# Cross-attention and quantised feed-forward: the order of two score products within a step

## The chip, the cores and the metric

The kernel runs on one core of a Trainium2 chip. The metric is the device time of one execution in microseconds (us); "before" is the median of three runs. PE is TensorE, DVE is VectorE, ACT is ScalarE, POOL is GpSimd, and SP is the queue that issues most transfers.

## The reference

The inputs are `x` and a context `ctx`, both 4 x 1024 x 512 in float32. What is computed, cut to what matters:

```
# per batch, N = 1024 tokens (768 image, then 256 text), 16 heads of 32
q = layernorm(x) @ Wq + bq;  k = ctx @ Wk + bk;  v = ctx @ Wv + bv
scores = q k^T / sqrt(32)
# mask: an image token sees its own third of the image (256 tokens);
#       a text token sees all the image and, causally, the text
attn = softmax(scores);  x = x + (attn @ v) @ Wo + bo
# feed-forward with fake quantisation to 8 bits of activations (one scale for
# the whole tensor) and of weights (one scale for each row), inner width 1408
x = x + down( quant( silu(gate(quant(layernorm(x)))) * up(...) ) )
```

## The kernel before

The program has three stages. Attention with its projections is the first, up to about 870 us of the span; the gate and up products of the feed-forward, up to about 1032 us, are the second; the down products are the third. The change lies in the first stage alone.

**Units and steps.** Queries are worked on in blocks of 256 tokens, and heads in four groups `g` of four. A `Unit` is one block of queries against one block of 256 keys, for one group of heads. An image block has one unit for each group; a text block has four (its `part` 0 to 3), since it looks at all four key blocks. There are 112 units. The main loop (lines 821 to 908) runs over steps `n`, and each step works on three units in a software pipeline:

- `maxima(units[n])` (lines 426 to 449) makes scores `s` with the queries on the partitions: eight products into four PSUM banks, one for each head of the group. DVE then takes the row maxima of each bank (L445 for image blocks, L449 for text blocks, after adding a mask at L448 where the block is causal). They become the shifts of the softmax: POOL rounds them to pairs of bf16 (`minus_maxima`, L465 and L466), and a transposing transfer lays them along the free axis (`shifts`, L473, tile `nmT`).
- `weights(units[n - T_LAG], ...)` (lines 476 to 516), five units behind, makes the scores once more with the keys on the partitions. Four small bf16 products (L488) put minus the maxima into four banks `t`, and eight products (L492) add the scores. ACT takes the exponentials (L494) into `pT`. The function that it returns, `sums`, adds them up on POOL (L514).
- `values(units[n - V_LAG])` (lines 518 to 572), six units behind, multiplies `pT` of the step before with the values (L532, bank `av`), and at the last part with a block of ones for the sums (L555).
- `large(n)` then does one larger piece: half of a projection of a coming block (tiles `pp_q`, `pp_kv`, `pv`) or of an output projection (`po`), all at L225. Its bank is called the large bank below. From step `LATE` on the pieces are half as large.

After these come, on DVE, whatever the step has of background work: the reciprocal of the sums (L567), a sum of terms for text blocks (L569 and L545), taking an output projection (L588) and its statistics (L595 to L598), the statistics of a new query block (L359, L360), scales of the weights of the feed-forward (L636 to L638), and the transposition of a new block of inputs (L260).

**What sets the order.** For PE, DVE, ACT and POOL the order is the program's own: `tc.manual_schedule` (line 777) takes the instructions of each engine as they are written. The transfers of SP are placed by the scheduler. So the order in which PE meets the products of one step is the order of the calls in the loop: `weights`, `maxima`, `values`, `large`.

**Banks.** All PSUM of the stage is one pool of eight banks with one tag:

```python
        def bank(name):
            return ps_b.tile([P, 512], F32, tag="b", name=name)
```

A step takes ten banks: four for `s`, four for `t`, one for `av`, one for the large piece. A product that takes a bank has to wait until its last reader, from the tile that held the bank before, is done. In the built program the bank numbers go round: almost always a tile takes the bank that was taken eight tiles earlier.

Of the kernel before, what the change touches and what calls it, by code (L numbers as in the profile page):

```python
# [42 lines left out]
def kernel(ctx: ExitStack, tc: tile.TileContext, x, kv, Wq, bq, Wk, bk, Wv, bv, Wo, bo, clip_x, clip_down, w_gate, w_up, w_down, out):  # L43
# [78 lines left out]
    with ExitStack() as actx:  # L122
# [9 lines left out]
        def bank(name):  # L132
            return ps_b.tile([P, 512], F32, tag="b", name=name)
# [267 lines left out]
        def rows_of(j):  # L401
            return slice(j * D, (j + 1) * D)
# [23 lines left out]
        def maxima(u):  # L426

            k, g = u.k, u.g
            q = Q[k.c]
            if u.part == 0:  # L430
                state[k.n, g] = small.tile([P, 4, 2, 2], F32, tag="nmh", name=f"nmh_{u.n}", bufs=4)
            nmh = state[k.n, g]
            s = [bank(f"s_{u.n}_{j}") for j in range(4)]
            i, half = u.part // 2, u.part % 2
            n = 2 * QB - (P if k.text and half and i == 0 else 0)
            for m in range(2):
                if k.text:
                    key, rows, w = K[k.keys[2 * half + m]], slice(i * P, (i + 1) * P), min(QB, n - m * QB)
                else:
                    key, rows, w = K[k.c], slice(m * P, (m + 1) * P), QB  # L440
                for j in range(4):
                    nc.tensor.matmul(s[j][:, m * QB : m * QB + w], q[rows_of(j), g, rows], key[rows_of(j), g, :w], start=True, stop=True)  # L442
            for j in range(4):
                if not k.text:
                    nc.vector.tensor_reduce(nmh[:, j, :, 0], s[j].rearrange("p (i q) -> p i q", i=2), AX.X, ALU.max, negate=True)  # L445
                    continue
                if half:
                    nc.vector.tensor_tensor(s[j][:, n - P : n], s[j][:, n - P : n], mask, ALU.add)  # L448
                nc.vector.tensor_reduce(nmh[:, j, i, half : half + 1], s[j][:, :n], AX.X, ALU.max, negate=True)  # L449
# [3 lines left out]
        def minus_maxima(u):  # L453

            k, g = u.k, u.g
            nmh = state.pop((k.n, g))
            if k.text:
                nm = small.tile([P, 4, 2], F32, tag="nm", name=f"nm_{u.n}")
                nc.vector.tensor_reduce(nm, nmh, AX.X, ALU.min)
            else:  # L460
                nm = nmh[:, :, :, 0]
            nm = nm.rearrange("p j i -> p i j")
            nm2 = nm2s[turn[0] % NMB]
            turn[0] += 1
            nc.gpsimd.tensor_copy(nm2[:, :, :, 0], nm)  # L465
            nc.gpsimd.tensor_tensor(nm2[:, :, :, 1], nm, nm2[:, :, :, 0], ALU.subtract)  # L466
            u.nm2 = nm2

        def shifts(u):

            k, g, nm2 = u.k, u.g, u.nm2
            nmT = nmp.tile([P, QB], BF16, tag="nmT", name=f"nmT_{u.n}")
            nc.sync.dma_start_transpose(nmT.rearrange("p (i q) -> p i q", i=2), nm2.rearrange("p i j d -> p (i j d)"))  # L473
            state["T", k.n, g] = nmT
# [176 lines left out]
        units = []  # L651
# [33 lines left out]
        def can_small(n):  # L685
            return at_small < len(jobs) and at_small <= at_big + 1 and prepared.get(at_small, n) < n
# [36 lines left out]
        def need_rows(kind, c, g, n):  # L723

            while rows_done.get((kind, c), 0) <= g:
                advance(n)

        def need_values(c, n):
            while ("v", c) not in done:
                advance(n)  # L730
# [9 lines left out]
        def step_output(half=False):  # L740
            outputs[0].step(half)
            if outputs[0].i == 2:
                outputs.pop(0)
                for o in outputs[:2]:
                    o.load()

        def finished(k):
            outputs.append(Output(k))
            for o in outputs[:2]:
                o.load()  # L750
# [70 lines left out]
        for n in range(len(units) + V_LAG):  # L821
            previous = units[n - 1] if 0 < n <= len(units) else None
            if n < len(units):
                u = units[n]
                half = u.part % 2
                for c in u.k.keys[2 * half : 2 * half + 2] if u.k.text else u.k.keys:
                    need_rows("k", c, u.g, n)
                need_rows("q", u.k.c, u.g, n)

            def shifts_of_previous():  # L830
                if previous is not None and previous.part == previous.parts - 1:
                    shifts(previous)

            if T_LAG <= n < len(units) + T_LAG:
                sums = weights(units[n - T_LAG], shifts_of_previous)
            else:
                shifts_of_previous()
                sums = None
            if n < len(units):
                maxima(u)  # L840
            if sums is not None:
                sums()
            if n < len(units) and u.part == u.parts - 1:
                minus_maxima(u)
            if n in (2, 3, 4, 5):
                (spread, sigmoids, product, total)[n - 2]()

            for first, c in ((True, (n - 5) // 3), (False, (n - 7) // 3)):
                rows = slice(c * QB, (c + 1) * QB)
                if not 0 <= c < B * NQB or (n - (5 if first else 7)) % 3:  # L850
                    continue
                if first:
                    nc.sync.dma_start(x1_d[rows, :].rearrange("(t p) c -> p t c", p=P), bo_b.unsqueeze(1).to_broadcast([P, QB // P, C]))
                else:
                    nc.gpsimd.dma_start(x1_d[rows, :], x_tok[rows, :], accum_op=ALU.add, max_dma_last_dim=C)
            t = units[n - T_LAG] if T_LAG <= n < LATE else None
            crowded = t is not None and t.k.text and t.part > 1
            while sum(b.__name__ == "moments" for b in background) > 1:
                background.popleft()()
            f = background.popleft() if background and n > 0 and not (crowded and background[0].__name__ == "deviation") else None  # L860
            if f is not None and f.__name__ in ("deviation", "apply", "quantise"):
                f()
                f = background.popleft() if background and f.__name__ == "quantise" else None
            fs = list(later)
            later.clear()
            for g in fs:
                g()
            ends = None
            if n >= V_LAG:
                v = units[n - V_LAG]  # L870
                need_values(v.k.keys[v.part], n)
                if v.part == 0 and v.g == 0:
                    while len(outputs) + len(whole) >= OUTS:
                        step_output()
                if v is units[-5]:
                    tail.load()
                ends = values(v)
            if ends is not None:
                avs, av, quotient = ends
                if n < len(units) + V_LAG - 1:  # L880
                    nc.scalar.copy(avs, av)
            large(n)
            while whole:
                finished(whole.pop(0))
            if f is not None:
                f()
            if ends is not None and n < len(units) + V_LAG - 1:
                later.append(quotient)
            if n == len(units) + V_LAG - 2:
                assert not outputs  # L890
                tail_products(0, (0, 1))

            if weight_stages and quantised[0]:
                weight_stages.popleft()()
            if can_small(n):
                small_step()
            prepare_next(n)
            if n > n_img and n_weights < 2 * NIC and not weight_stages and len(background) < 2:
                stages = weight_unit(n_weights)
                background.extend(stages[:2])  # L900
                weight_stages.append(stages[2])
                n_weights += 1
            if n < LATE and spent + BIG < target(n) and can_big(n + 1):
                big_step()
            if n >= V_LAG:
                u = units[n - V_LAG]
                if u.part == u.parts - 1 and u.g == NCC - 1 and u is not units[-1]:
                    whole.append(u.k)
# [306 lines left out]
```

## Time and profile before

| what | value |
|---|---|
| median of three runs | 1118.52 us (1116.16 to 1120.01) |
| the profiled execution's own time | 1117.18 us |
| its span, first to last instruction | 1115.3 us |
| mean granted TensorE clock | 0.987 |
| PE busy | 1087.0 us, 97% of the span |
| DVE busy | 846.9 us, 76% |
| ACT busy | 522.1 us, 47% |
| POOL busy | 531.0 us, 48% |

The profile has a page of busy times, groups of instructions by source line, and a chain of work that ended last; the trace behind it can be asked for the instructions of an engine in order of time. A row of the timeline gives the start in us, the time taken, the engine, the line, the operation, what it writes and reads, and the number of instructions merged into the row. In brackets stands idle time of the engine before it, with what ended it. A product in float32 is recorded as two matmuls, so the eight products of `s` appear as sixteen. The table by windows gives for each stretch of time the busy time of each engine and, after the engines, the granted clock of PE as a share of full speed.

### The profile page before, as it was taken

The numbers are of one execution on the slowest core, as the hardware profiler recorded it, in microseconds if no ns is written. First come the engines' busy times: TensorE is split into PE (matmuls) and PEld (weight loads), VectorE is DVE, ScalarE is ACT, GpSimd is POOL, SyncE is SP. The second block draws the span as 40 slices with busy tenths as digits, with TensorE's granted clock in tenths as the row PEclk, the third lists the DMA queues.
The fourth block names the chain that finished last, engine by engine and source line by source line (L and its number), as shares of the span: only waits on it lengthen the run. The fifth ranks groups of instructions, "written<-read, shape, count | busy, mean of one in ns | idle before, by whom it ended". The sixth has DMA issues, their size and how long they took to land.

```text
span 1115.3 us, 32159 instructions
## 1 busy us (share of the span) xinstructions
PE 1087.0 (97%) x13851; PEld 585.9 (53%) x13851; DVE 846.9 (76%) x1316; ACT 522.1 (47%) x941; POOL 531.0 (48%) x615
## 2 busy tenths in 40 slices
PE   9998999999999999999999999989999899998998
PEld 5555555465655555565545556655554344443444
DVE  2555678797688959778786887987777788877887
ACT  3344444354445435454533455554443565553653
POOL 1224447678764567775446666765642221110110
PEclk9998999999999999999999999998999899999999
DMA  7369636355645454332222122212211698311895
GB/s 236 93 202 284 144 80 133 72 117 102 121 63 115 94 117 85 108 82 65 92 73 67 42 77 61 60 53 80 72 66 58 203 287 247 75 34 39 300 382 193
DMA packets 138262, 135.91 MB, mean 122 GB/s; under 512 B 56060, under 2 KB 103432, under 8 KB 136712
## 3 DMA queue, kind: packets, MB, share of 16 engines
q1 hardware_dynamic: 115600, 91.91, 29.6%
q0 software_dynamic: 22208, 41.42, 14.1%
q8 instruction: 108, 1.77, 0.7%
q10 hardware_dynamic: 312, 0.53, 0.2%
q14 instruction: 34, 0.28, 0.1%
HBM read 79.96 MB, written 50.07 MB: 117 GB/s over the span
## 4 chain that ended last, share of the span: by engine, by line
PE 81%; DMA 6%; DVE 5%; POOL 3%; issue 2%; ACT 2%; SPq 1%; DVEq 0%; POOLq 0%; ACTq 0%
PE po L225 9%; PE av L532 8%; PE pv L225 8%; PE pp_q L225 8%; PE pp_kv L225 8%; PE s L442 8%; PE t L492 7%; PE pg L1055 7%; PE pu L1055 7%; PE t L488 3%; PE av L555 3%; PE pd L1158 2%; POOL sp L514 2%; DMA xt<-x_d 2%; ACT pT L494 1%
## 5 line engine op out<-in xcount | busy, mean ns | idle before, releaser
L494 ACT ACTIVATE pT<-t 128x512 f32<-128x512 f32 x448 | 231.3, 603 | 135.7 <-PE t L492 135.5
L514 POOL TENSOR_TENSOR sp<-pT 128x1024 f32<-128x1024 f32 x59 | 140.8, 2386 | 173.8 <-ACT pT L494 173.7
L514 POOL TENSOR_TENSOR sp<-sp,pT 128x1024 f32<-128x1024 f32 x84 | 188.8, 2248 | 46.8 <-ACT pT L494 43.5
L449 DVE TENSOR_REDUCE nmh<-s 128x1 f32<-128x512 f32 (+1 forms) x256 | 159.2, 655 | 46.7 <-PE s L442 42.3
L445 DVE TENSOR_REDUCE nmh<-s 128x2 f32<-128x512 f32 x192 | 119.0, 683 | 58.9 <-PE s L442 58.9
L442 PE MATMUL s<-kT,qT 32*128 32x256 f32 (+1 forms) x1792 | 128.5, 376 | 3.1 <-DVE xr L588 2.5
L532 PE MATMUL av<-pT,va 128*32 128x256 f32 (+1 forms) x1792 | 118.9, 383 | 1.7 <-ACT pT L494 1.4
L225 PE MATMUL pp_q<-qT,Wq_sb 128*32 128x256 f32 x2048 | 117.4, 379 | 0.0
L225 PE MATMUL pv<-Wv_sb,kvT 128*32 128x512 f32 (+1 forms) x1088 | 116.3, 567 | 0.0
L492 PE MATMUL t<-qT,kT 32*128 32x256 f32 (+1 forms) x1792 | 115.1, 371 | 0.0
L225 PE MATMUL po<-Wo_sb,oT 128*32 128x512 f32 (+1 forms) x1120 | 110.9, 536 | 0.0
L567 DVE RECIPROCAL avs<-avs 128x256 f32<-128x256 f32 x63 | 109.9, 1744 | 0.0
L225 PE MATMUL pp_kv<-kvT,Wk_sb 128*32 128x256 f32 x1920 | 109.0, 379 | 0.0
L442 PEld LDWEIGHTS s<-kT,qT 32*128 32x128 f32 x1792 | 99.0, 187 | 16.1 <-DVE xr L588 3.4
L492 PEld LDWEIGHTS t<-qT,kT 32*128 32x128 f32 x1792 | 89.6, 186 | 7.2 <-issue 0.7
L1055 PE MATMUL pg<-xqT,wgT 128*128 128x512 bf16 x352 | 91.0, 382 | 0.5 <-DVE xqT L1016 0.5
L225 PEld LDWEIGHTS pp_q<-qT,Wq_sb 128*32 128x32 f32 x2048 | 67.7, 110 | 44.9 <-issue 3.6
L1055 PE MATMUL pu<-xqT,wuT 128*128 128x512 bf16 x352 | 90.6, 381 | 0.0
L1061 ACT ACTIVATE silu<-pg,sg 128x512 f32<-128x512 f32 x88 | 60.0, 686 | 64.9 <-PE pg L1055 64.9
L1082 DVE SCALAR_TENSOR_TENSOR h<-pu,su,silu 128x512 f32<-128x512 f32 x88 | 65.4, 747 | 30.2 <-PE pu L1055 29.2
L225 PEld LDWEIGHTS pp_kv<-kvT,Wk_sb 128*32 128x32 f32 x1920 | 63.8, 110 | 42.7 <-issue 4.5
L532 PEld LDWEIGHTS av<-pT,va 128*32 128x32 f32 x1792 | 48.6, 110 | 56.7 <-ACT pT L494 27.2
(190 smaller groups left out, 1340.5 us busy)
## 6 DMA issues: line engine op xcount, KB each, us to landing
xt<-x_d SPq DMA_DIRECT2D x16, 1024.0 KB, 6.4
h<-h_d POOLq DMA_DIRECT2D x3, 2816.0 KB, 13.7
xb<-in_x_dram SPq DMA_DIRECT2D x16, 512.0 KB, 4.3
x_d<-bo_b SPq DMA_DIRECT2D x16, 512.0 KB, 7.0
x_d<-in_x_dram POOLq DMA_DIRECT2D x16, 512.0 KB, 6.8
xr<-x_d SPq DMA_DIRECT2D x16, 512.0 KB, 3.7
x_d<-xr POOLq DMA_DIRECT2D x16, 512.0 KB, 3.3
spread_kv<-in_ctx_dram SPq DMA_DIRECT2D x60, 128.0 KB, 3.0
```

Of the source, the lines that this page charges most:

```text
L225: nc.tensor.matmul(out[rows_of(j)], lhs[:, rows_of(j)], rhs, start=start, stop=stop, tile_position=(0, j * D), skip_group_check=True)
L442: nc.tensor.matmul(s[j][:, m * QB : m * QB + w], q[rows_of(j), g, rows], key[rows_of(j), g, :w], start=True, stop=True)
L445: nc.vector.tensor_reduce(nmh[:, j, :, 0], s[j].rearrange("p (i q) -> p i q", i=2), AX.X, ALU.max, negate=True)
L449: nc.vector.tensor_reduce(nmh[:, j, i, half : half + 1], s[j][:, :n], AX.X, ALU.max, negate=True)
L492: nc.tensor.matmul(t[j][:, n, cols], kc[rows_of(j), g, n * P : (n + 1) * P], q[rows_of(j), g, cols], start=False, stop=(n == 1))
L494: nc.scalar.activation(pT[:, j], t[j], AF.Exp)
L514: nc.gpsimd.tensor_tensor(sp[:, :, cols], a, pT[:, :, n, cols], ALU.add)
L532: nc.tensor.matmul(av[rows_of(j), 0, cols], va[:, n, g * P + j * D : g * P + (j + 1) * D], u.pT[:, j, n, cols], start=(n == 0), stop=(n == 1),
L567: nc.vector.reciprocal(avs[:, 1, :], avs[:, 1, :])
L1055: nc.tensor.matmul(ps, w[:, cc, ic * P : (ic + 1) * P], qT[:, cc, :], start=(cc == 0), stop=(cc == NCC - 1))
L1061: nc.scalar.activation(s, pg, AF.Silu, scale=sg[:, ic : ic + 1])
L1082: nc.vector.scalar_tensor_tensor(h[:, ic, :], pu, su[:, ic : ic + 1], s, ALU.mult, ALU.mult)
```

## The change

Within a step, `maxima(u)` is called ahead of `weights(...)` and `shifts_of_previous` in place of behind them. Nothing is added or taken away; `values`, `large` and all background work stay where they were.

```diff
@@ -831,13 +831,13 @@
                 if previous is not None and previous.part == previous.parts - 1:
                     shifts(previous)
 
+            if n < len(units):
+                maxima(u)
             if T_LAG <= n < len(units) + T_LAG:
                 sums = weights(units[n - T_LAG], shifts_of_previous)
             else:
                 shifts_of_previous()
                 sums = None
-            if n < len(units):
-                maxima(u)
             if sums is not None:
                 sums()
             if n < len(units) and u.part == u.parts - 1:
```

In the built programs the order of DVE's, ACT's and POOL's instructions is the same before and after. On PE the sixteen records of `s` stand ahead of `t` where they stood behind. Since the pool hands out its banks in the order of the calls, the tiles of a step also land in other banks.

## The prediction

> **What bounds the kernel now.** I read the page first. PE is busy for 97% of the span, and DVE, with 76%, is the next. The two groups of row maxima show that DVE mostly waits for PE's scores, 46.7 and 58.9 us in all, and `av` and `s` show next to no idle time of PE:
>
> ```profile
> PE 1087.0 (97%) x13851; PEld 585.9 (53%) x13851; DVE 846.9 (76%) x1316; ACT 522.1 (47%) x941; POOL 531.0 (48%) x615
> L449 DVE TENSOR_REDUCE nmh<-s 128x1 f32<-128x512 f32 (+1 forms) x256 | 159.2, 655 | 46.7 <-PE s L442 42.3
> L442 PE MATMUL s<-kT,qT 32*128 32x256 f32 (+1 forms) x1792 | 128.5, 376 | 3.1 <-DVE xr L588 2.5
> L532 PE MATMUL av<-pT,va 128*32 128x256 f32 (+1 forms) x1792 | 118.9, 383 | 1.7 <-ACT pT L494 1.4
> ```
>
> So the first stage is a chain of PE's products with little room. Averages hide, however, that DVE is far behind PE in some steps. The timeline of PE, three steps of a text block, shows a rigid rhythm: bias, `t`, `s`, `av`, large piece, and again.
>
> ```profile
> 209.90 0.40 PE L488 MATMUL t<-nmT,onesb 2*128 2x512 bf16 x4
> 210.12 1.03 PE L492 MATMUL t<-qT,kT 32*128 32x256 f32 x16
> 210.99 1.03 PE L442 MATMUL s<-kT,qT 32*128 32x256 f32 x16
> 211.95 1.07 PE L532 MATMUL av<-pT,va 128*32 128x256 f32 x16
> 212.84 3.62 PE L225 MATMUL pv<-Wv_sb,kvT 128*32 128x512 f32 x32
> ...
> 222.88 0.40 PE L488 MATMUL t<-nmT,onesb 2*128 2x512 bf16 x4
> ...
> 225.92 1.07 PE L532 MATMUL av<-pT,va 128*32 128x256 f32 x16
> ```
>
> `s` starts 1.09 us after its step, and `av` 2.05 us after it. The timeline of DVE over the same steps:
>
> ```profile
> 210.02 0.69 DVE L588 TENSOR_TENSOR xr<-po,xr 128x512 f32<-128x512 f32 x1 [1.59 <-PE po L225]
> ...
> 212.02 0.68 DVE L598 TENSOR_REDUCE xm<-xr 128x1 f32<-128x512 f32 x1
> 212.61 2.47 DVE L449 TENSOR_REDUCE nmh<-s 128x1 f32<-128x512 f32 x4
> ...
> 219.87 0.68 DVE L598 TENSOR_REDUCE xm<-xr 128x1 f32<-128x512 f32 x1
> ...
> 225.82 2.18 DVE L260 STREAM_TRANSPOSE kvT<-spread_kv 128x1024 f32<-128x1024 f32 x1
> 227.92 2.46 DVE L449 TENSOR_REDUCE nmh<-s 128x1 f32<-128x512 f32 x4
> ```
>
> From 210.02 on DVE never rests. It comes free for the maxima of the steps at 209.90, 216.38 and 222.88 at 212.70, 220.55 and 228.00: 2.80, 4.17 and 5.12 us after the start of the step. Today that costs little, because the banks of `s` are wanted late.
>
> **What the change moves: banks.** With ten tiles a step on a ring of eight, the order of the calls decides who waits for whom. Before, `av` takes the bank of the same step's first `t`, the large piece that of the second, the last two `t` take the first two `s` banks of the step before, and the last two `s` the banks of `av` and the large piece. After, `av` takes the bank of the same step's first `s` and the large piece that of the second. In the built programs the first product of `av` waits for ACT before and for DVE after. Before, the maximum of the first head had until the next step's third `t`, 4.5 us after `av` starts; after, it has to be done before `av` can start at all, and all of PE's products queue behind `av`.
>
> **The cost of a late DVE.** PE wants `av` 2.05 us after the step's start, as now (the same products come ahead of it). The first maximum takes 0.69 us (1.02 with the mask), plus about 0.05 for the signal. On time this fits: the maxima can start 1.06 us into the step and end at 1.8, or 2.0 with the mask. If DVE comes free at 2.80, `av` waits 2.80 - 0.03 + 0.68 + 0.05 - 2.05 = 1.44 us. I took this sum for each step that the timeline shows. 59 of 104 are late, by 119 us together. But they must not be added, because a wait of PE lets DVE catch up: over a stretch in which DVE never rests, the total is the largest lateness, here 3.94 at 222.88, not 1.44 + 3.14 + 3.94. And a stretch that began with DVE waiting for `s` begins 1.09 us earlier after the change, so 1.09 comes off; one that began with something else (L588, L260) gets no such start. The waits per stretch, by time in the span:
>
> - 72 to 130: 12.30. The step at 89.39 has a transposition (L260) ahead of its maxima that waits for a transfer until 101.11.
> - 130 to 203: 3.13, 0.80, 1.15; sum 5.08.
> - 203 to 407, a whole batch: 3.94, 1.04, 2.86, 0.83, 0.47, 0.86, 1.20, 0.80, 1.16; sum 13.16.
> - 407 to 611, the next: 13.88.
> - 611 to 700: 3.14, 0.91, 2.53, 0.27; sum 6.85.
> - 700 to 868, where large pieces are halved and a step takes 4.8 us: 1.10, 3.53, 2.76, 2.76, 0.15, 3.65, 0.07, 1.26; sum 15.28.
>
> Together 66.6 us.
>
> **What goes away.** The same lateness costs something now: `s` or the bias products start late because banks of `s`, `av` or a `po` are not free. Against the rhythm these steps lose 6.9 us (at 99.81), 1.9 to 2.0 in each of the three stretches of time from 203 to 700, and 12.9 after 700; 25.7 in all. After the change PE has then already waited for DVE at `av`. Two waits for `nmT` (1.42 at 663.85, 1.30 at 731.25) go too, since the maxima are ready 1.09 us earlier and their use comes 0.87 later. Gain 28.4 us.
>
> **Clock.** A longer wait also slows PE afterwards. The one long wait for L588 and what follows:
>
> ```profile
> 795.39 1.14 PE L442 MATMUL s<-kT,qT 32*128 32x256 f32 x10 [2.50 <-DVE xr L588]
> ```
>
> ```profile
> 796.00:800.00 4.00, 4.00 (x42) 1.82 (x41) 4.00 (x8) 0.00 (x0) 3.92 (x3) 0.57 0.08 16
> ```
>
> The granted clock is 0.57 over these 4 us, so 0.43 x 4 = 1.7 us are lost after a wait of 2.50 us; the waits near 1 us at 222.88 and 276.51 leave the clock at 1.00 over 130 to 300. Five new waits of 2.5 us or more stand where no slow clock stands now (3.13, 2.86, 2.89, 3.53, 2.76): 5 x 1.7 = 8.6 us. Bounds are 0 and, at 3.4 us each (0.43 x 8, as after 772), 17 us; I take the nearest row, the wait of 2.50 us.
>
> [...]
>
> **Edits at nothing.** The exponentials start about 1 us later in the step; ACT idles 135.7 us over 112 steps waiting for `t`, 1.2 us a step, and `pT` is read by `values` a whole step later. If that cover were gone it would cost up to 1 us a step. The sums on POOL (2.2 to 2.4 us each) shift with them; their reader, L555, comes more than 9 us later. The second maximum ends 0.62 us (0.93 masked) after the first, under the 0.89 us of `av`. The last two `t` now need the banks of `av` and the large piece 0.1 to 0.2 us earlier than the last two `s` did; ACT's take of a large bank (0.84) just fits; without that margin 0.1 x 47 steps, 5 us. On SP the transposing transfers keep their place behind POOL's shifts and change places only with initial copies to `x_d`; those are needed many steps later.
>
> **Sum.** 66.6 - 28.4 + 8.6 = +46.8 us. On the profiled execution's 1117.18 us this gives 1164; the median of the runs is 1.3 us above it, so 1165. About 0.3% (3.4 us) is what a measurement of this kernel can tell from no change.
>
> **Rivals.** First, *DVE catches up more than I allow*: the work that starts a stretch is itself early, so all stretches gain the 1.09 us, and no clock is lost. That takes 14.7 from the new waits: 66.6 - 14.7 - 28.4 = +23.5, 1142. For it speaks that PE's waits leave DVE time before the next release; against it that L588 and L260 wait for the end of the large piece, which does not move.
>
> Second, *faster*: the waits that go away (28.4 us) outweigh the new ones. This is the mechanism of the 1.09 us head start alone; it decides once the maxima come about another 1.1 us earlier in each of the 35 stretches, which cuts 66.6 to 28.4. With no new wait at all the time would be 1118.5 - 28.4 = 1090. The 105 us that DVE waits for `s` speak for it: where it waits it is on time. Against it are the 59 late steps. Near the balance, no change.
>
> Third, *nothing is caught up*: DVE's work in a stretch waits for PE anyway, so each late step pays in full: 119 - 28.4 + 8.6 = +99, 1218. The rows without any idle time of DVE speak against it.
>
> **How the numbers follow.** Forecast 0.55, at 1165 (1150 to 1190, the top with half of the catching up lost: 26 us). First rival 0.30, 1128 to 1150. Third 0.08. Second 0.05, and 0.02 for no change. A range of 1140 to 1190 leaves out the third, the second and part of the first. Slower 0.93, same 0.02, faster 0.05.
>
> **What would show it.** Right: in the profile after, idle time before `av` L532 named for DVE's maxima (L445, L449, L448) of tens of us, where ACT stood with 1.4; the step at 222.88 and its like in each batch with waits of 4 us in two or three pieces; gate, up and down stages unchanged in length; the idle time of DVE before the maxima smaller or moved. Wrong: PE's rhythm unchanged at `av`, or `av` waiting for ACT. If the batch from 203 to 407 grows by under 5 us, the first rival holds; by over 20, the third.

## The result and the profile after

The changed kernel takes 1165.28 us (median of five runs, 1163.06 to 1167.7) against 1118.52: 1.0419 times as long, with a 95% interval of 1.0396 to 1.0442. The profiled execution took 1166.66 us; its span is 1164.9 us, 49.6 us more than before, at a mean granted clock of 0.982. Attention holds all of it: the first gate product starts at 921.99 us where it started at 872.33 us, the gate and up stage takes 160.62 us after 160.31, the down stage 82.33 us after 82.65.

The page of the changed kernel, with its busy times and three groups:

```profile
PE 1093.2 (94%) x13829; PEld 588.6 (51%) x13851; DVE 840.5 (72%) x1316; ACT 519.8 (45%) x941; POOL 529.7 (45%) x615
L449 DVE TENSOR_REDUCE nmh<-s 128x1 f32<-128x512 f32 (+1 forms) x256 | 159.0, 652 | 50.0 <-PE s L442 45.6
L532 PE MATMUL av<-pT,va 128*32 128x256 f32 (+1 forms) x1792 | 120.2, 386 | 52.4 <-DVE nmh L449 30.8
L442 PE MATMUL s<-kT,qT 32*128 32x256 f32 (+1 forms) x1792 | 125.2, 393 | 0.0
```

The idle time before `av` went from 1.7 to 52.4 us and changed its releaser from ACT to DVE; the 3.1 us before `s` are gone. The maxima of the text blocks wait for `s` about as long as before (50.0 us, then 46.7). So PE now waits for DVE in some steps, and DVE for PE in others. PE's waits in the table of waits (total us, times, the longest):

```profile
PE av L532 <- DVE nmh L449: 30.8, 26, 4.3
PE av L532 <- DVE nmh L445: 19.3, 11, 9.1
PE pbt L206 <- DVE nmh L445: 1.8, 1, 1.8
```

37 waits make 50.1 us of the 52.4. The third line belongs to a step that has no `av`: there a product of the output bias takes the bank in its place. The first waits of the batch that in before starts near 203 us, in the timeline of PE after:

```profile
230.71 1.07 PE L532 MATMUL av<-pT,va 128*32 128x256 f32 x16 [1.23 <-DVE nmh L449]
231.60 3.62 PE L225 MATMUL pv<-Wv_sb,kvT 128*32 128x512 f32 x32
235.15 1.15 PE L442 MATMUL s<-kT,qT 32*128 32x256 f32 x16
236.11 0.40 PE L488 MATMUL t<-nmT,onesb 2*128 2x512 bf16 x4
236.33 1.04 PE L492 MATMUL t<-qT,kT 32*128 32x256 f32 x16
237.51 1.07 PE L532 MATMUL av<-pT,va 128*32 128x256 f32 x16
244.84 1.07 PE L532 MATMUL av<-pT,va 128*32 128x256 f32 x16 [0.81 <-DVE nmh L449]
```

The three `av` are those that stood at 211.95, 218.44 and 225.92. DVE over the same time, after:

```profile
227.39 0.69 DVE L588 TENSOR_TENSOR xr<-po,xr 128x512 f32<-128x512 f32 x1 [2.67 <-PE po L225]
...
229.98 2.47 DVE L449 TENSOR_REDUCE nmh<-s 128x1 f32<-128x512 f32 x4
232.37 1.74 DVE L567 RECIPROCAL avs<-avs 128x256 f32<-128x256 f32 x1
234.03 0.42 DVE L569 TENSOR_TENSOR avs<-avs,oT 128x256 f32<-128x256 f32 x1
...
242.14 2.07 DVE L260 STREAM_TRANSPOSE kvT<-spread_kv 128x1024 f32<-128x1024 f32 x1 [0.47 <-PE pv L225]
244.15 2.44 DVE L449 TENSOR_REDUCE nmh<-s 128x1 f32<-128x512 f32 x4
```

The first of four maxima starts at 229.98 and takes some 0.65 us; `av` starts at 230.71, 0.73 us after its start. This is the mechanism of the prediction: `av` starts when DVE has read the first bank of `s`. Likewise 244.15 and 244.84.

### The profile page after: what moved, and what is told of

Same layout as the page of the kernel before. It is cut to its first block, busy times and chain, and to the rows that moved or that the text cites. A ratio compares the mean times of both kernels' runs of the same rounds, so it can differ in the third digit from the quotient of the medians.

```text
span 1164.9 us, 32187 instructions
## 1 busy us (share of the span) xinstructions
PE 1093.2 (94%) x13829; PEld 588.6 (51%) x13851; DVE 840.5 (72%) x1316; ACT 519.8 (45%) x941; POOL 529.7 (45%) x615
## 4 chain that ended last, share of the span: by engine, by line
PE 70%; DVE 16%; issue 4%; POOL 4%; DMA 3%; ACT 1%; SPq 1%; DVEq 0%; POOLq 0%; ACTq 0%
PE po L225 9%; PE av L532 7%; PE pv L225 7%; PE pp_kv L225 7%; PE pp_q L225 7%; PE pg L1055 7%; PE pu L1055 6%; PE s L442 6%; PE pd L1158 5%; PE t L492 4%; DVE nmh L449 3%; POOL sp L514 3%; PE av L555 2%; DVE avs L567 2%; DVE kvT L260 2%
## 5 line engine op out<-in xcount | busy, mean ns | idle before, releaser
L494 ACT ACTIVATE pT<-t 128x512 f32<-128x512 f32 x448 | 231.3, 603 | 211.7 <-PE t L492 208.5
L514 POOL TENSOR_TENSOR sp<-pT 128x1024 f32<-128x1024 f32 x59 | 140.6, 2383 | 222.0 <-ACT pT L494 214.3
L514 POOL TENSOR_TENSOR sp<-sp,pT 128x1024 f32<-128x1024 f32 x84 | 188.8, 2247 | 67.0 <-ACT pT L494 63.7
L532 PE MATMUL av<-pT,va 128*32 128x256 f32 (+1 forms) x1792 | 120.2, 386 | 52.4 <-DVE nmh L449 30.8
L445 DVE TENSOR_REDUCE nmh<-s 128x2 f32<-128x512 f32 x192 | 118.7, 681 | 62.2 <-PE s L442 62.2
L442 PE MATMUL s<-kT,qT 32*128 32x256 f32 (+1 forms) x1792 | 125.2, 393 | 0.0
L225 PE MATMUL pp_q<-qT,Wq_sb 128*32 128x256 f32 x2048 | 121.3, 388 | 0.0
L442 PEld LDWEIGHTS s<-kT,qT 32*128 32x128 f32 x1792 | 80.8, 184 | 64.4 <-issue 54.1
L225 PE MATMUL pp_kv<-kvT,Wk_sb 128*32 128x256 f32 x1920 | 111.7, 385 | 0.0
L492 PEld LDWEIGHTS t<-qT,kT 32*128 32x128 f32 x1792 | 92.0, 184 | 19.4 <-issue 11.7
L225 PEld LDWEIGHTS pp_kv<-kvT,Wk_sb 128*32 128x32 f32 x1920 | 67.0, 112 | 42.8 <-issue 8.4
## 6 DMA issues: line engine op xcount, KB each, us to landing
h<-h_d POOLq DMA_DIRECT2D x3, 2816.0 KB, 13.6
```

Of the source, the lines that this page charges most:

```text
L225: nc.tensor.matmul(out[rows_of(j)], lhs[:, rows_of(j)], rhs, start=start, stop=stop, tile_position=(0, j * D), skip_group_check=True)
L492: nc.tensor.matmul(t[j][:, n, cols], kc[rows_of(j), g, n * P : (n + 1) * P], q[rows_of(j), g, cols], start=False, stop=(n == 1))
L494: nc.scalar.activation(pT[:, j], t[j], AF.Exp)
L514: nc.gpsimd.tensor_tensor(sp[:, :, cols], a, pT[:, :, n, cols], ALU.add)
L532: nc.tensor.matmul(av[rows_of(j), 0, cols], va[:, n, g * P + j * D : g * P + (j + 1) * D], u.pT[:, j, n, cols], start=(n == 0), stop=(n == 1),
```

## The experiments

**The order and the bank, one at a time (e1, e2).** The change does two things: it moves `s` ahead of `t`, and by the ring of banks it gives `av` a bank of `s` in place of one of `t`. Both experiments name the bank of `av` and of the large piece by hand, from eight tags of one bank each; other tiles take the bank that was taken longest ago. e1 has the order of after and the banks of `t`, e2 the order of before and the banks of `s` (`mine["s"]` where e1 has `mine["t"]`).

```diff
+        def bank(name, like=None):
+            i = free[0] if like is None else like
+            free.remove(i); free.append(i)
...
+            return ps_b.tile([P, 512], F32, tag=f"b{i}", name=name, bufs=1)
-            av = bank(f"av_{u.n}")
+            av = bank(f"av_{u.n}", mine["t"][0])
+            mine["large"] = mine["t"][1]
```

> The order of after (s ahead of t), but av takes the bank of the same step's first t and the large piece that of the second, as before; the next step's s takes the four s banks of the step before. The outputs are the same. Theory (whose reader frees av's bank): no wait of av for DVE is left; instead av waits in every step for ACT's first exponential. In the trace of before the exponentials start 1.13 us after t and one takes 0.60, so t's first bank is free 1.75 us after t starts, and av is wanted 0.97 after it: about 0.8 us in each of some 105 steps, 84 us, plus a rhythm that is 0.1 us a step longer than before (11 us, seen in after), less up to 25 us of old waits: about 1185 (1170 to 1200), idle time before av named for the exponentials. Rival (the order itself costs the time, whoever holds the bank): within 10 us of after, 1155 to 1175, and idle time before av still named for DVE or gone.

> The order of before (t ahead of s), but av takes the bank of the same step's first s and the large piece that of the second; the next step's t takes the four t banks. The outputs are the same. Theory (bank): av waits for DVE in every step, since the first maximum ends 1.06 + 0.69 + 0.05 = 1.80 us after s starts and av is wanted 0.99 after it: 0.8 us in 105 steps, 0.3 more where the mask is added first, 95 us, plus what the late steps need beyond that, 30 to 60 us, less 28 of old waits: about 1225 (1195 to 1250). Rival (the order itself): the order is that of before, so within 10 us of 1118.

Measured in three rounds each: e1 1182.6 us, ratio 1.0574 (1.0534 to 1.0614); e2 1220.57 us, ratio 1.0918 (1.0877 to 1.0959).

| us | `av` takes a bank of `t` | `av` takes a bank of `s` |
|---|---|---|
| `t` first, `s` second | 1118.52 (before) | 1220.57 (e2) |
| `s` first, `t` second | 1182.6 (e1) | 1165.28 (after) |

The page of e1 and the one of e2, the group of `av`:

```profile
L544 PE MATMUL av<-pT,va 128*32 128x256 f32 (+1 forms) x1792 | 116.5, 377 | 74.8 <-ACT pT L504 74.0
```

```profile
L544 PE MATMUL av<-pT,va 128*32 128x256 f32 (+1 forms) x1792 | 120.2, 386 | 119.2 <-DVE nmh L459 71.2
```

In e1 the new wait is ACT's and stands in nearly every step. Its timelines of PE and of ACT, one step:

```profile
410.57 1.07 PE L544 MATMUL av<-pT,va 128*32 128x256 f32 x16 [0.69 <-ACT pT L504]
```

```profile
409.92 2.07 ACT L504 ACTIVATE pT<-t 128x512 f32<-128x512 f32 x4 [1.33 <-PE t L502]
```

The exponentials start when `t` is there, 0.65 us before `av`, and `av` goes when the first is done. In e2 the wait is DVE's (119.2 us), because `s` comes just ahead of `av` and even a punctual maximum is too late. No run names the banks by hand with the order and the banks of before, so what the naming itself costs is not measured. Both runs came within what was expected of the theory, and outside the rival's. So neither part explains the result by itself. Whichever scores come last are not read yet when `av` wants their bank: taking the bank of the first scores of the step is the better choice in both rows. What is left to pay then is the delay of the reader: 1.7 us for ACT, which is hardly ever late, and 52.4 us for DVE, which often is.

**Whether the waits come from DVE's other work (e3, e4).** In both kernels the statistics of the rows after attention (L595 to L598, some 2.2 us of DVE at a time) are left out, and constants stand in their place.

```diff
                 def moments():
-                    st = small.tile([P, 6], F32, tag="st2", name=name)
...
+                    pass
-    nc.gpsimd.memset(xm2, 0.0)
+    nc.gpsimd.memset(xm2, 2.0)
```

> After, with the statistics of the attention's output (L595 to L598, 2.2 us on DVE, thirty times) left out; the scale of the feed-forward then comes from a constant. Theory (DVE comes late to the maxima because of background work ahead of them): the waits of av for DVE shrink by a third to a half, 15 to 25 us, mostly in steps that follow an output projection: 1140 to 1150. Rival (DVE's maxima are too slow in any step, or the clock does it): less than 8 us of change.

> Before, with the same statistics left out: the control for the run without them after the change. Theory: banks of s are wanted late in this order, so DVE's work is hidden except in the few steps with old waits: 1108 to 1117. If it falls by 15 us or more, the statistics cost the same in both orders and the lateness is not what the change exposed.

Measured in three rounds: e3 1150.79 us, ratio 1.0293 (1.0255 to 1.033), 0.8 us above the upper end of what was expected; e4 1116.04 us, ratio 0.997 (0.995 to 0.9989). The page of e3:

```profile
L532 PE MATMUL av<-pT,va 128*32 128x256 f32 (+1 forms) x1792 | 118.2, 381 | 37.9 <-DVE nmh L449 23.3
```

The same work of DVE costs 14.5 us after and some 3 us before. The idle time before `av` falls by as much (52.4 to 37.9 us), in a profile whose span is 17.5 us shorter. So the order of after pays for DVE's background work, most of which the order of before hid.

**The slow sum of DVE (e5, e6).** The trace had one row that was not understood when the prediction was written: L569, a sum of two tiles of 128x256, took anything from 0.36 to 2.46 us. The timelines of before, of DVE and of POOL:

```profile
243.37 2.39 DVE L569 TENSOR_TENSOR avs<-avs,oT 128x256 f32<-128x256 f32 x1
```

```profile
240.65 4.83 POOL L514 TENSOR_TENSOR sp<-sp,pT 128x1024 f32<-128x1024 f32 x2 [1.27 <-ACT pT L494]
```

POOL's row holds two sums and ends at 245.48, L569 at 245.76. In both traces each L569 that starts within a sum of L514 ends 0.28 to 0.29 us behind that sum; the four of before that start outside take 0.36 to 0.51 us. e5 moves L569 to POOL in the kernel before, e6 in the one after.

```diff
-                        nc.vector.tensor_tensor(avs[:, 0, :], avs[:, 0, :], o, ALU.add)
+                        nc.gpsimd.tensor_tensor(avs[:, 0, :], avs[:, 0, :], o, ALU.add)
```

> Before, with the sum of terms for text blocks (L569, 16 of them) moved from DVE to POOL; the outputs are the same. In before these 16 take 28.9 us of DVE, 1.9 to 2.5 us each where one starts inside a POOL sum (L514), and 0.36 to 0.51 elsewhere. Theory (late DVE, hidden by this order except for the old waits, most of which stand after a step with L569): some of the 28 us of old waits go, 1110 to 1118. Rival (DVE's lateness costs nothing before): within 2 us of before; slower if POOL, busy for 48%, then holds up the sums that av needs.

> After, with the same sum moved to POOL; the outputs are the same. In after the 16 take 24.0 us of DVE, ahead of the next maxima in most steps. Theory: waits of av for DVE fall by more than in the run with the order of before, by 6 to 14 us, to 1151 to 1159; the idle time before av, 52.4 in after, falls to about 42. Rival (the lateness is not DVE's queue): under 3 us.

Measured in five rounds: e5 1109.81 us (1108.95 to 1115.1) beside 1117.69 for before, ratio 0.9934 (0.9913 to 0.9955), 0.2 us below the range that was expected; e6 1155.57 us, ratio 1.0343 (1.032 to 1.0367). e5 is faster than both kernels of the case. In the groups by line of e5:

```profile
L569 POOL TENSOR_TENSOR avs<-avs,oT 128x256 f32<-128x256 f32 x16 | 12.8, 799 | 0.0
```

28.9 us of DVE have become 12.8 us of POOL. In e6 the idle time before `av` is 40.5 us, 11.9 less than after.

**The rhythm (e7, e8, e9).** A step without a wait takes longer after than before. The 16 records of `s` start within 0.772 us (before 0.659): the first four take 0.478 us each where they took 0.374. From the start of a step without a wait to its large piece it is 3.046 us against 2.941 (medians). The weight loads of these four records start 0.002 us ahead of them; in before all sixteen loads start 0.21 us ahead (medians). The author's guess from these medians: with the large piece just ahead of `s` the first loads don't start early, and with some 0.2 us of small products ahead they would. e7 tried the bias products ahead of `s`, on top of e1:

```diff
+            if T_LAG <= n < len(units) + T_LAG:
+                shift_products(units[n - T_LAG])
             if n < len(units):
                 maxima(u)
```

> The run of after's order with av on t's bank, but with the four small bias products (L488 in before) ahead of s: bias, s, t. The outputs are the same. Question: why a step without any wait is 0.10 us longer after the change. In before and in the run with before's order the sixteen records of s start within 0.66 us, in both runs with s first within 0.77. Theory (the first weight loads of s can't run ahead under the large piece, while those of the bias products are short): with the bias first, s takes 0.66 again. Rival (the order of s and t, or the banks): 0.77. The time itself is of less use, since the banks of the bias products are then wanted earlier: 1175 to 1215.

One run: 1209.29 us. `s` waited for banks (11.3 us) and its records mix with those of `t`, so the starts from first to last say nothing here. The records one by one do: the first six, behind the bias products, take 0.37 to 0.38 us each, and the four behind a wait for a bank take 0.478 us; the page has 391 ns as the mean of all, where after has 393 and before 376. e8 and e9 put four other small products into the banks of `s`, ahead of it; `s` overwrites what they leave there. e8 uses 16 columns, e9 512.

```diff
             s = [bank(f"s_{u.n}_{j}") for j in range(4)]
...
+            for j in range(4):
+                nc.tensor.matmul(s[j][:, :16], ones_j, ones_j[:, :16], start=True, stop=True)   # e8
+                nc.tensor.matmul(s[j], ones_j, ones_j.to_broadcast([2, 4, P]), start=True, stop=True)   # e9
```

(e8 has the first of the two products, e9 the second; `ones_j` is short for `onesb[j * D : j * D + 2, :]`.)

> After, with four small bf16 products (2 rows by 128, 16 columns) written into the four s banks just ahead of s, which overwrites them; the outputs are the same. Question: why s takes 0.77 us in after from its first to its last start and 0.66 in before. In after the first four products of s take 0.478 us and the others 0.374, and their weight loads (0.18 us) start with them; in before the loads run 0.2 us ahead, under t. Theory (the first weight loads are not hidden behind the large piece): behind the small products, whose own loads are short (0.09), the loads of s run ahead again, all its products take 0.374, and the sixteen start within 0.66. Rival (the banks or the change of the array's tiling cost it): 0.77 as in after. The small products cost some 0.2 us a step themselves, so the time is 1160 to 1185 either way.

> As the run before this one, but the small products have 512 columns, as the bias products have, in place of 16. There the small products lasted 0.03 us, too short to cover a weight load of 0.18 us, and s still took 0.74 from its first to its last start. Theory (the first weight loads of s need some 0.2 us of cover by products of the same tiling): the cover is now 0.2 us, as in before, and the sixteen starts of s stand within 0.66 us, all its products at 0.374. Rival: 0.74 to 0.77 again, so the cause lies elsewhere. The step itself gets 0.1 us longer (0.22 for the small products, less 0.11): 1170 to 1185.

One run each: e8 1164.72 us, e9 1170.86 us. e8 missed: its products are records of 178 ns (in e9 386), and `s` still takes 0.744 us from first to last start, with 397 ns as the mean of one product. In e9 `s` starts within 0.660 us, as before. The groups by line and shape, after and then e9 (mean ns of one product: before 384 with its waits):

```profile
L442 PE MATMUL s<-kT,qT 32*128 32x256 f32 x1664 | 121.4, 402 | 0.0
```

```profile
L445 PE MATMUL s<-kT,qT 32*128 32x256 f32 x1664 | 108.9, 374 | 0.0
```

Timelines of PE, one step of after and the same one of e9:

```profile
414.40 1.15 PE L442 MATMUL s<-kT,qT 32*128 32x256 f32 x16
```

```profile
413.47 0.40 PE L438 MATMUL s<-onesb 2*128 2x512 bf16 x4
413.70 1.03 PE L445 MATMUL s<-kT,qT 32*128 32x256 f32 x16
```

The small products take 0.23 us to win back 0.11, and e9 is not faster than after (one run, 5.6 us above its median). But with 0.2 us of small products ahead, the records of `s` are short again, 374 ns on the mean: that much is shown. Why the first loads start late behind the large piece was not shown; in e7 the four records behind a wait for a bank took 0.478 us too.

## Why the prediction was right, and where its terms were off

The forecast of 1165 us and the mechanism were right: `av` waits for DVE's maxima, the feed-forward stages did not change, and the batch from 203 to 407 us grew by 11.3 us, between the marks of 5 and 20 us that would have spoken for the first and the third rival. The sum is nearer than its terms are, though, and that part is luck: two terms were 12.4 and 5.5 us too high, one of 11.2 us was left out, and the gain was 9.5 us too large, which nearly cancels. Forecast and measured, in us:

| term | forecast | measured | from |
|---|---|---|---|
| new waits | +66.6 | +54.2 | idle before `av` 52.4, before `pbt` 1.8 |
| slower clock after waits | +8.6 | +3.1 | half of the time at half clock with PE at work: 22.9 us of attention, before 16.8 |
| rhythm of a step | 0 | +11.2 | 0.105 a step, some 107 steps |
| lateness that goes | -28.4 | -18.9 | the remainder, not measured by itself |
| sum | +46.8 | +49.6 | difference of the spans |

What each stage added to the delay of `av` against before (stages by the times of before, us; the forecast is the stage's new waits and lost clock less what goes away in it):

| stage | up to 130 | 130 to 203 | 203 to 407 | 407 to 611 | 611 to 700 | 700 to 868 |
|---|---|---|---|---|---|---|
| forecast | 5.4 | 6.8 | 12.9 | 13.6 | 3.5 | 4.5 |
| measured | 7.0 | 10.3 | 11.3 | 11.2 | 4.2 | 5.6 |

**The rhythm: the step that failed.** "PE wants `av` 2.05 us after the step's start, as now (the same products come ahead of it)" counts the products and takes their duration to be the same in any order. The trace of before showed that it is not, in the steps at 51.69 and 56.36, where the large piece and not `t` stands ahead of `s`; its timeline of PE, one step without and one with `t`:

```profile
56.36 1.15 PE L442 MATMUL s<-kT,qT 32*128 32x256 f32 x16
...
66.43 1.06 PE L442 MATMUL s<-kT,qT 32*128 32x256 f32 x16
```

Behind `t` `s` takes 1.03 to 1.06 us, without it 1.15. 0.1 us a step is 11 us in all, nearly as much as the largest miss.

**The new waits: 12 us too high.** The rule of the largest lateness held in its form: in the stretch of 222.88 the three waits are 1.23, 0.14 and 0.81 us, 2.18 together, in the two or three pieces that were named. The forecast was 3.94. L569 took 1.90 us in the second step before and 0.42 us after (234.03), since POOL's sum ended 0.14 us after its start: 1.48 of the 1.76 us that are missing. A chain of DVE's rows was carried over with durations that depended on another engine. L569 fell from 28.9 to 24.0 us over the kernel. The largest single miss is the step whose `av` stood at 91.47: 9.13 us where 12.30 was forecast. Others went either way: 4.33 where 3.13 was forecast (133.83), 1.99 where it was 2.86 (272.05). In the two longest waits DVE itself stood waiting for transfers, as its timeline after shows:

```profile
98.59 0.69 DVE L359 BATCH_NORM_STATS2 st<-xb 128x6 f32<-128x512 f32 x1 [8.76 <-DMA xb<-in_x_dram]
142.67 2.02 DVE L260 STREAM_TRANSPOSE qT<-spread_q 128x1024 f32<-128x1024 f32 x1 [4.16 <-DMA spread_q<-xn_d]
```

Behind the first row the transposition starts at 100.32, 0.8 us earlier than before (101.11), while its step had come 2.15 us later (91.54, before 89.39). The forecast's sum carries the lateness of before over unchanged, as if the transfer moved with the step. Two steps, at 387 and 592, waited 1.00 us each where the rule said none, so it isn't exact.

**What goes away.** The direction was right: the waits of `s` and of the bias products for banks and for `nmT` are gone (`nmT`: 2.7 to 0.2 us). The remainder of the sum puts it at 18.9 us, 9.5 less than forecast; no run measures it by itself.

**Clock.** The term was 5.5 us too high. The windows of after:

```profile
150.00:300.00 150.00, 142.47 (x2147) 78.69 (x2139) 109.01 (x191) 64.60 (x130) 95.99 (x88) 1.00 0.44 95
791.37:794.78 3.41, 1.31 (x28) 0.61 (x24) 3.25 (x9) 2.67 (x5) 3.33 (x4) 1.00 0.02 5
794.78:798.19 3.41, 3.41 (x36) 1.72 (x31) 2.09 (x5) 0.00 (x0) 3.33 (x2) 0.50 0.34 79
293.02:296.43 3.41, 2.12 (x40) 1.33 (x44) 3.41 (x7) 2.04 (x4) 2.79 (x3) 1.00 0.23 57
```

The waits of 9.13 and 4.33 us brought 10.24 and 6.83 us at half clock, those near 775, 794, 818 and 843 (2.94, 2.10, 2.11, and 1.24 with 1.34 us within 4 us) 3.41 us each; other waits, of up to 1.99 us, brought none. But half clock also set in while a wait still lasted: in 7.8 of these 30.7 us PE had no work, and there it cost nothing.

Where it sets in can be read from the trace. The six stretches start at 98.46, 142.83, 774.30, 794.78, 818.67 and 842.57 us, which are 13, 185, 6, 7 and 7 times 3.413 us apart. So in this trace they all stand on one grid of 3.413 us. From 60 us to the end of attention, each window of this grid at full clock in which PE idled for 1.85 us or more was followed by one at half clock, and none with 1.61 us or less was. The wait of 2.10 us lies within one window (791.37), the one of 1.99 us at 294.31 across two, with 0.70 and 1.29 us in them (293.02). The two waits near 843 lie in one window, with 2.17 us of idle time together. The two figures hold for this trace alone: a window of before with 1.23 us (769.07), two waits with single small products between them, was followed by half clock as well.

The clock was 1.00 from 150 to 300 us, with waits of 0.5 to 2 us in it.

**Edits at nothing.** ACT's idle time before the exponentials grew from 135.7 to 211.7 us and nothing waited for them: the cover held. No product of `t` waited for ACT, the reader of `av`; two waited for L588, the reader of the large bank, 2.1 us in all, where before `s` had waited 2.5 us for it. One sign did not come: DVE's idle time before the maxima was to be smaller or moved, and grew by 3.3 us in both groups (46.7 to 50.0 and 58.9 to 62.2). One step was overlooked, the bias product `pbt` with its 1.8 us.

**Slips in the working.** A punctual maximum over 512 masked columns ends at 1.06 + 1.02 + 0.05 = 2.13 us, past the 2.05 and not at 2.0. The 0.93 us of a masked second maximum are not under the 0.89 us of `av`. The sum as printed gives 3.77 us for the step at 222.88; 3.94 is near what comes out if the shorter `t` of that step (0.82 us) is allowed for. And the second rival takes 1.1 us also off stretches that wait less than that. All are small beside the terms of the table.

**The rivals.** The second was wrong about DVE being on time: e4 and e3 show what its other work costs, some 3 us before and 14.5 after. The third, with 119 us of new waits, is out. The first put the new waits at 51.9 us, and the measured 54.2 lie nearer to that than to the forecast's 66.6; it is the rhythm, which neither had, that brings the time back to the forecast. The sign held all the same: without the rhythm, some 2.9 us in its 28 steps, the batch from 203 to 407 us would have grown by some 8.4 us. L569 and the transfer explain a part of the missing waits; whether DVE also caught up more than was allowed stays open.

## What to carry to other kernels

Where tiles take banks from a ring, the order of the calls also decides whose reader holds up whom: list for each tile the last reader of the bank that it takes, and when that reader is done. Here the best bank was that of the scores made first in the step, in both orders, and of the two orders the one in which their reader is hardly ever late. Before moving a group of products, look in the trace for the same group behind another neighbour; its duration there is the one to use. A duration that varies without a change of shape may depend on another engine, as that of L569 did, and then it must not be carried over into a new order.

## What the hardware showed that was not expected

- The first products of a group took another time with another neighbour ahead of them: 0.478 us for each of the first four records of `s` behind the large piece, with weight loads 0.002 us ahead of them; 0.374 behind `t` (before), with loads 0.21 us ahead; 0.374 on the mean behind small products of some 0.2 us (e9); 0.478 again behind a wait for a bank (e7).
- DVE's sum L569 took up to 2.46 us where it started inside a sum of POOL (L514), and 0.36 to 0.51 us where it did not (before); in both traces each of those that started inside ended 0.28 to 0.29 us after that sum. What holds it was not shown; e5 and e6 only have the sum on POOL.
- In the trace of after the six stretches at half clock in attention started whole multiples of 3.413 us apart. A wait of 2.10 us inside one window of that grid (791.37) was followed by half clock; one of 1.99 us across two (293.02), with 0.70 and 1.29 us in them, was not.
